# A ring of half-tick decays in PSUM, a second score bank, and operands laid out in half-tick slots

## The chip, the cores and the metric

The kernel runs on one core of one Trainium2 chip. The metric is the device time of one launch in microseconds (us), lower is better. The core has a matrix engine (TensorE, PE in the profile; its weight loads are listed apart as PEld), a vector engine (VectorE, DVE), an activation engine (ScalarE, ACT), a general engine (GpSimd, POOL) and a queue that issues transfers (SyncE, SP). Each engine takes its instructions strictly in the order in which they were written. Matrix products land in PSUM, eight banks of 128 partitions x 512 floats.

## The reference, cut to what matters

```python
# x: (4, 128, 64, 64): four images, 128 channels, 4096 pixels
x = x + attention(gn(x))        # 4096 x 4096 scores, softmax, values
x = x + conv5x5(gn(x))          # weights built from a radial table
x = x + ssm(gn(x))              # see below
x = x + conv3x3(gn(x))

# ssm: half of the channels runs forward over the pixels, half backward
xc    = silu(conv1d_4taps(Wx @ x))
delta = softplus(xc @ Wd + bd);  Bm = xc @ WB;  Cm = xc @ WC     # 64 states
h[t]  = exp(delta[t] * A) * h[t-1] + delta[t] * xc[t] * Bm[t]    # per channel and state
y[t]  = sum_n h[t, n] * Cm[t, n] + D * xc[t];  out = Wp @ y
```

`gn` is a group norm over 32 groups of 4 channels. All arithmetic is float32.

## The kernel before, in words

The scan of the state-space layer is the long part: 64 channels x 64 states x 2 directions are 64 sets of 128 rows, each 4096 pixels long, for four images. `scan_core` cuts this into **ticks**: one tick is one set of 128 rows over `CH` = 1024 pixels, 256 ticks an image, 1024 in all. A tick `i` has five steps, each on one engine:

- `drive(i + 2)`, L711, GpSimd: `db` = `dx` x `b` row (both in SBUF).
- `decay(i + 1, h)`, L704, ScalarE: `da` = exp(delta x A), written to PSUM. `da` has two buffers of two banks each, so a whole tick fits one buffer. While `attending` is set the decay is issued as two halves of 512, one at the tick's start and one in its middle, else as one instruction of 1024.
- `recur(i)`, L718 and L722, VectorE: a `tensor_tensor_scan` over 1024 pixels, and for 3 of 5 ticks (2 of 3 in the last image) the multiplication by the `c` row; in the other ticks GpSimd multiplies (`weigh`, L736).
- `keep(i - 1)`, L731, ScalarE: copies the last column of the state, the start value for the next 1024 pixels.
- `collect(i - 3)`, L750, TensorE: sums 4 states into a channel with 32-column products.

Everything else is written as generators. `front(b)` is attention, the 5x5 convolution and `scan_prep`/`scan_operands` of image `b`; `stage`, `end` and `back` finish an image after its scan. `front(0)` is written out first, alone. Then `scan_core` gives control away twice a tick, and the driver loop takes steps of the remaining work until their costs (the numbers that the generators yield: `PRODUCT` = 0.86 for one 128x512 product, `HOP` = 1.8 for a change of engine) have used up half of `pace`. `pace` is the summed cost of the first front divided by 248 ticks, so `front(b + 1)` is spread over the 256 ticks of image `b`. In the last image the pace is `ENDPACE` = 1.5 and the work is `stage`/`end`/`back` of the first three images.

PSUM before: 2 x 2 banks for `da`, and one bank each under the tags `s`, `a`, `z` and `y` (the last for `collect`).

**Attention** (L377 to L470) goes over 256 steps `u`, 32 blocks of keys for each of 8 blocks of queries: `scores(u)` (L380) multiplies into the bank `s`, ScalarE takes exp of it into an SBUF ring (L386), `values(u - 1)` (L392) adds the previous step's product to `a`, and every fourth step `sums` (L402) adds four steps' row sums in 32-column products. A float32 product is two matmul instructions with a weight load each. In TensorE's order a step is: scores(u), values(u - 1), sums now and then, and the scan's `y` products.

**Operands** (L538 to L651): for each of 8 pieces of 512 pixels, `taps` (16 matmuls into bank `s`), `halves` (L571, L572: half of the value to `xc`, tanh in place in PSUM), `silu` (L576, VectorE, from PSUM and `xc`), three products (L585: delta into `z`, the b and c rows one after the other into `a`), `softplus` (relu and abs, L598, L599), exp (L637), `digits` (L608 to L610) and two `row` copies (L590) with a DMA each. After the fourth and the eighth piece come the logarithms (L647, with a table load before and after) and `finish`: joins (L615), the DMA of delta, delta x xc on GpSimd into `xc` (L619) and its DMA. The next image's attention takes the buffer of `xc` (tag `A`) for its normalised input (L307).

Of the kernel before, what the change touches and what calls it, by code (L numbers as in the profile page):

```python
# [32 lines left out]
P = 128  # L33
# [10 lines left out]

PRODUCT, HOP, ENDPACE, SPARE, AHEAD = 0.86, 1.8, 1.5, 8, 4

# [5 lines left out]
def conv_preact_kernel(  # L52
# [36 lines left out]
    ps = ctx.enter_context(tc.tile_pool(name="ps", bufs=1, space=PSUM))  # L89
    pools, ready, attending = {}, set(), set()  # L90

    def bank(tag, name):
        return ps.tile([P, MM], F32, tag=tag, name=name)

# [172 lines left out]
    def group_norm(st, name):  # L267
# [29 lines left out]
        nc.vector.transpose(back.rearrange("p a b -> p (a b)"), after)  # L297
        yield HOP
        rs, nb = tile("rs", 1), tile("nb", 1)
        nc.gpsimd.tensor_tensor(rs, back[:, 0, 0:1], mhalf, ALU.pow)  # L300
        nc.gpsimd.tensor_tensor(nb, back[:, 1, 0:1], rs, ALU.mult)
        yield HOP
        yield HOP
# [15 lines left out]
    def attention(b, xs, gn, st, safe):  # L319
        xn = pools["big"].tile([P, ASIZE], F32, tag="A", name=f"xn0_{b}")[:, :L]  # L320
        for i in range(4):
            cut = bass.ts(i, L // 4)
            normalise(xn[:, cut], xs[:, cut], gn)
            yield HOP
        v = pools["big"].tile([P, VSIZE], F32, tag="V", name=f"v_{b}")
        v = v[:, : NJT * C].rearrange("p (j c) -> p j c", c=C)
        for i in range(NM):
            pv = bank("saz"[i % 3], f"pv_{b}_{i}").rearrange("p (t c) -> p t c", c=C)
            for t in range(TPM):
                nc.tensor.matmul(  # L330
                    pv[:, t, :], xn[:, bass.ts(i * TPM + t, P)], wv,
                    start=True, stop=True,
                )
            nc.scalar.copy(v[:, i * TPM : (i + 1) * TPM, :], pv)
            yield 2 * PRODUCT

# [40 lines left out]
        def scores(u):  # L377
            blk, j = divmod(u, NJT)
            sc = bank("s", f"sc_{b}_{u}")
            nc.tensor.matmul(sc, xn[:, bass.ts(j, P)], rq[blk], start=True, stop=True)  # L380
            pt = ring[:, u % NRING, :]
            if safe:
                nc.vector.tensor_tensor(pt, sc, mb[blk], ALU.subtract)
                nc.scalar.activation(pt, pt, AF.Exp)
            else:
                nc.scalar.activation(pt, sc, AF.Exp)  # L386
# [44 lines left out]
        def settle(blk):  # L431
# [6 lines left out]
            nc.vector.bn_stats(st[:, blk, :], xs[:, cut])  # L438

        queries(0)  # L440
        attending.add(b)
        for u in range(N + 7):
            blk, j = divmod(u, NJT)
            cost = 0.0
            if u < N:
                if safe and j == 0:
                    row_max(blk)
                scores(u)
                cost += PRODUCT
            if 0 < u <= N:  # L450
                values(u - 1)
                cost += PRODUCT
                d = (u - 1) % NJT
                if d == 3:
                    after(u, 3, sums, u - 1)
                elif d % 4 == 3:
                    sums(u - 1)
                    cost += PRODUCT
                if d == NJT - 1:
                    evict(blk - 1)  # L460
                    after(u, 2, turn, blk - 1)
                    after(u, 5, settle, blk - 1)
            if j == 16 and blk + 1 < NM:
                queries(blk + 1)
                cost += PRODUCT
            for f, args in later.pop(u, ()):
                f(*args)
                cost += PRODUCT
            yield cost or HOP
        attending.clear()  # L470


    def conv(b, xs, tag, st, weights, k, finish, name, residual=False):
# [16 lines left out]

        for i in range(2):
            piece(i)
            yield HOP
        done = None
# [26 lines left out]
    def scan_prep(b, xs, st, mats4):  # L521


        bc, dd, dxd, xcd, xsd = mats4
        pad = KC - 1
        xn = pools["big"].tile([P, VSIZE], F32, tag="V", name=f"xn2_{b}")
        nc.gpsimd.memset(xn[:, :pad], 0.0)
        nc.gpsimd.memset(xn[:, pad + L : 2 * pad + L], 0.0)
        gn = yield from group_norm(st, f"s{b}")

        for i in (0, 3, 1, 2):
            cut = slice(i * L // 4, (i + 1) * L // 4)
            normalise(xn[:, pad + cut.start : pad + cut.stop], xs[:, cut], gn)
            nc.sync.dma_start(xsd[:, cut], xs[:, cut])
            yield HOP
        return scan_operands(b, xn, mats4)

    def scan_operands(b, xn, mats4):  # L538

# [6 lines left out]
        delta = pools["big"].tile([P, L], F32, tag="xt", name=f"delta_{b}")  # L546
        pts, pzs, pbs, us = {}, {}, {}, {}

        def taps(i):
            pts[i] = pt = bank("s", f"pt_{b}_{i}")  # L550
            t = i * MM
            for k in range(KC):
                lo = L + 2 * pad - 1 - k - t - (MM - 1)
# [14 lines left out]
        def halves(i):  # L568

            pt = pts[i]  # L570
            nc.scalar.activation(xc[:, bass.ts(i, MM)], pt, AF.Identity, scale=0.5, bias=hbias)  # L571
            nc.scalar.activation(pt, pt, AF.Tanh, scale=0.5, bias=hbias)  # L572

        def silu(i):
            cut = bass.ts(i, MM)
            nc.vector.scalar_tensor_tensor(  # L576
                xc[:, cut], pts.pop(i), 1.0, xc[:, cut], ALU.add, ALU.mult
            )
# [32 lines left out]

        def finish(c):
            for i in range(c * CH // MM, (c + 1) * CH // MM):
                cut = bass.ts(i, MM)
                nc.vector.tensor_tensor(delta[:, cut], delta[:, cut], us.pop(i), ALU.add)  # L615
            cut = bass.ts(c, CH)
            nc.sync.dma_start(dd[c], delta[:, cut])
            yield HOP
            nc.gpsimd.tensor_tensor(xc[:, cut], delta[:, cut], xc[:, cut], ALU.mult)  # L619
            nc.sync.dma_start(dxd[c], xc[:, cut])  # L620
            yield HOP

        for i in range(NM + 1):
            if i < NM:
                taps(i)
                yield KC * PRODUCT
                halves(i)
            if i > 0:
                pzs[i - 1] = product(i - 1, 0, "z")
                yield PRODUCT  # L630
                pbs[i - 1, 1] = product(i - 1, 1, "a")
                softplus(i - 1)
            if i < NM:
                silu(i)
            if i > 0:
                yield PRODUCT
                nc.scalar.activation(pzs[i - 1], pzs[i - 1], AF.Exp, scale=-1.0)  # L637
                row(i - 1, 1)
                yield PRODUCT
                pbs[i - 1, 2] = product(i - 1, 2, "a")  # L640
                digits(i - 1)
                yield PRODUCT
                row(i - 1, 2)
            if i > 0 and i % HM == 0:
                yield HOP
                for n in range(i - HM, i):
                    nc.scalar.activation(us[n], us[n], AF.Ln)  # L647
                yield HOP
                for c in range((i - HM) * MM // CH, i * MM // CH):
                    yield from finish(c)  # L650
                ready.add((b, i))  # L651

# [3 lines left out]
    def scan_core(mats4, ynds, before):  # L656
# [5 lines left out]
        ]  # L662
        rows, rep, exps, dbs, hcs, hold, yacc, xcs, last = {}, {}, {}, {}, {}, {}, {}, {}, {}
        whole = {}

# [28 lines left out]

        def decay(i, h):

            b, c, d, q, g = ticks[i]
            if h == 0:
                exps[i] = ps.tile([P, CH], F32, tag="da", bufs=2, name=f"da_{i}")
                whole[i] = not attending  # L700
            elif whole.pop(i):
                return
            cut = slice(None) if h == 0 and whole[i] else bass.ts(h, MM)
            nc.scalar.activation(  # L704
                exps[i][:, cut], rep["de", b, c, d, g][:, cut], AF.Exp, scale=a_neg[:, at(i)]
            )
# [6 lines left out]
        def recur(i):  # L713
            b, c, d, q, g = ticks[i]
            hc = pools["hc"].tile([P, CH], F32, tag="hc", name=f"hc_{i}")
            da = exps.pop(i)
            h = hc if to_pool(i) else da
            nc.vector.tensor_tensor_scan(  # L718
                h, da, dbs.pop(i), 0.0 if c == 0 else last[b][:, at(i)], ALU.mult, ALU.add
            )  # L720
            if not to_pool(i):
                nc.vector.tensor_tensor(hc, h, rows["c", b, c, d, q], ALU.mult)  # L722
            hcs[i], hold[i] = hc, h

        def keep(i):
            b, c, d, q, g = ticks[i]
            h = hold.pop(i)
            if b not in last:
                last[b] = small.tile([P, NK * NQ], F32, tag="last", name=f"last_{b}")
            if c + 1 < NCH:  # L730
                nc.scalar.copy(last[b][:, at(i)], h[:, CH - 1 : CH])  # L731

# [294 lines left out]
```

## Time and profile before

| | |
|---|---|
| median of 3 runs | 5047.01 us (5046.7 to 5051.97) |
| the profiled execution | 5047.28 us, span of the profile 5045.2 us |
| instructions | 41640 |
| busy in the span | PE 86%, DVE 70%, ACT 45%, POOL 67% |
| granted TensorE clock | 0.928 |

The stages, by where the trace has the first and last instruction of each:

| stretch (us) | what runs |
|---|---|
| 0 to 40 | constants, first image, group norm, v of image 0 |
| 40 to 604 | attention of image 0, alone |
| 611 to 787 | 5x5 convolution of image 0, alone |
| 787 to 892 | operands of image 0, alone; the first tick's scan starts at 891.8 |
| 892 to 4116 | ticks of images 0, 1, 2, with the fronts of images 1, 2, 3 beside them: attention 898 to 1544, 1943 to 2592 and 2991 to 3638; convolution 1564 to 1773, 2618 to 2827 and 3662 to 3871; operands, group norms and the opening of attention between |
| 4116 to 4947 | ticks of image 3, with the ends of images 0 to 2 beside them |
| 4947 to 5045 | the end of image 3 alone |

Idle time of an engine costs something only where that engine sets the pace of its stretch; so the table of stretches has to be read with the busy time of each engine beside it. Matmuls are pipelined, so their recorded times overlap, and a busy PE can still lose time between two of them: for that the start times are to be compared.

### The profile page before, as it was taken

How to read it: one execution, taken by the hardware profiler on the slowest of the kernel's cores; microseconds unless marked ns; L12 is line 12 of the kernel's file. 1: busy time of each engine (PE TensorE's matmuls, PEld its weight loads, DVE VectorE, ACT ScalarE, POOL GpSimd, SP SyncE). 2: the span in 40 equal slices, each digit the busy share in tenths (PEclk: the TensorE clock that was granted, in tenths of full speed). 3: DMA queues.
4: the chain of work that ended last, by engine and by line, in shares of the span. 5: the costliest groups of instructions: out<-in, count | busy, mean ns of one | idle time of the engine just before them, and what ended most of it. 6: DMA issues, size and time to landing. Idle time of an engine off the chain costs nothing. (4 is left out here: it accounts for less than half of the span.)

```text
span 5045.2 us, 41640 instructions
## 1 busy us (share of the span) xinstructions
PE 4328.1 (86%) x14288; PEld 1484.1 (29%) x14288; DVE 3513.6 (70%) x2359; ACT 2261.0 (45%) x3843; POOL 3357.7 (67%) x1516
## 2 busy tenths in 40 slices
PE   7999996999998968999989869999999675858547
PEld 3333342333333312333323223333333121212102
DVE  5000003777778887777788887777788999999993
ACT  2322203655554345555553455555533544444331
POOL 0000000777778877777778777787788889999992
PEclk9999999999999989999999989999999797878668
DMA  1000003434444465444344554444444656565651
GB/s 44 0 0 0 0 4 118 162 135 144 151 148 149 152 215 177 149 139 153 130 156 149 193 186 145 144 149 144 151 156 165 248 179 225 196 229 201 209 189 49
DMA packets 208398, 710.90 MB, mean 141 GB/s; under 512 B 24624, under 2 KB 25520, under 8 KB 208048
## 3 DMA queue, kind: packets, MB, share of 16 engines
q1 hardware_dynamic: 206432, 706.83, 40.4%
q8 instruction: 114, 1.87, 0.2%
q10 hardware_dynamic: 1744, 1.32, 0.1%
q14 instruction: 108, 0.88, 0.1%
HBM read 640.94 MB, written 67.11 MB: 140 GB/s over the span
## 5 line engine op out<-in xcount | busy, mean ns | idle before, releaser
L711 POOL TENSOR_TENSOR db<-dx,br 128x1024 f32<-128x1024 f32 x1024 | 2405.3, 2364 | 597.0 <-DVE hc L718 255.2
L704 ACT ACTIVATE da<-de,a_neg 128x512 f32<-128x512 f32 (+1 forms) x1497 | 1267.4, 847 | 410.8 <-DVE hc L722 290.8
L718 DVE TENSOR_TENSOR_SCAN da<-da,last,db 128x1024 f32<-128x1024 f32 x474 | 1111.7, 2345 | 187.5 <-ACT da L704 167.9
L380 PE MATMUL sc<-r,xn 128*128 128x512 f32 x2048 | 1146.7, 642 | 40.2 <-ACT pt L386 19.7
L386 ACT ACTIVATE pt<-sc 128x512 f32<-128x512 f32 x1024 | 610.4, 596 | 1022.3 <-PE sc L380 1021.9
L392 PE MATMUL acc<-pt,v 128*128 128x512 f32 x2048 | 1046.4, 593 | 0.0
L750 PE MATMUL y<-hc,sel 128*32 128x512 f32 x4096 | 690.0, 675 | 409.0 <-POOL hc L736 379.5
L736 POOL TENSOR_TENSOR hc<-hc,cr 128x1024 f32<-128x1024 f32 x392 | 927.8, 2367 | 96.1 <-ACT last L731 93.0
L722 DVE TENSOR_TENSOR hc<-da,cr 128x1024 f32<-128x1024 f32 x632 | 774.1, 1225 | 54.0 <-issue 0.9
L502 PE MATMUL pce<-xpe,cw 128*128 128x512 f32 x1600 | 723.9, 606 | 40.0 <-ACT xpe L307 40.0
L718 DVE TENSOR_TENSOR_SCAN hc<-da,last,db 128x1024 f32<-128x1024 f32 x294 | 688.7, 2343 | 76.5 <-ACT da L704 51.7
L392 PEld LDWEIGHTS acc<-pt,v 128*128 128x128 f32 x2048 | 389.1, 190 | 491.4 <-issue 487.4
L380 PEld LDWEIGHTS sc<-r,xn 128*128 128x128 f32 x2048 | 305.2, 188 | 768.1 <-ACT pt L386 363.1
L718 DVE TENSOR_TENSOR_SCAN da<-da,db 128x1024 f32<-128x1024 f32 x158 | 361.9, 2290 | 147.1 <-ACT da L704 125.8
L502 PEld LDWEIGHTS pce<-xpe,cw 128*128 128x128 f32 x1600 | 298.6, 191 | 465.0 <-issue 420.9
L480 POOL MEMSET xpe<- 128x136 f32 x4 | 0.8, 211 | 569.1 <-PE sc L380 569.1
L750 PEld LDWEIGHTS y<-hc,sel 128*32 128x32 f32 x4096 | 103.6, 114 | 892.0 <-POOL hc L736 511.8
L426 DVE COPY zall<-pz 128x4 f32<-128x4 f32 x32 | 5.1, 160 | 497.6 <-PE pz L422 497.5
L731 ACT COPY last<-da 128x1 f32<-128x1 f32 x473 | 74.4, 157 | 576.4 <-DVE hc L722 575.7
L502 PE MATMUL pcm<-xpm,m 128*128 128x512 f32 x576 | 283.3, 640 | 23.5 <-ACT xpm L307 23.5
L402 PE MATMUL zp<-pt,ones 128*32 128x512 f32 x2048 | 272.7, 605 | 0.0
L718 DVE TENSOR_TENSOR_SCAN hc<-da,db 128x1024 f32<-128x1024 f32 x98 | 223.7, 2283 | 42.0 <-ACT da L704 34.2
(160 smaller groups left out, 1865.3 us busy)
## 6 DMA issues: line engine op xcount, KB each, us to landing
br<-bm SPq DMA_DIRECT2D x512, 512.0 KB, 5.1
cr<-cm SPq DMA_DIRECT2D x512, 512.0 KB, 4.0
de<-dd SPq DMA_DIRECT2D x64, 512.0 KB, 4.8
dx<-dxd SPq DMA_DIRECT2D x64, 512.0 KB, 6.1
x<-in_x_dram SPq DMA_DIRECT2D x16, 512.0 KB, 5.9
xsd<-x SPq DMA_DIRECT2D x16, 512.0 KB, 6.2
xcd<-xc SPq DMA_DIRECT2D x16, 512.0 KB, 2.7
bm<-bs SPq DMA_DIRECT2D x32, 256.0 KB, 2.2
```

Of the source, the lines that this page charges most:

```text
L380: nc.tensor.matmul(sc, xn[:, bass.ts(j, P)], rq[blk], start=True, stop=True)
L386: nc.scalar.activation(pt, sc, AF.Exp)
L392: nc.tensor.matmul(acc[blk], v[:, j, :], ring[:, u % NRING, :], start=j == 0, stop=j == NJT - 1)
L402: nc.tensor.matmul(zp[blk][g * 32 : (g + 1) * 32, :], ones[:, :32], ring[:, (u - 3 + g) % NRING, :], start=j == 3, stop=j == NJT - 1, tile ...
L502: nc.tensor.matmul(acc.rearrange("p (r w) -> p r w", w=W), weights[:, t, :], xp[:, y : y + RPM, dx : dx + W], start=t == 0, stop=t == k * ...
L704: nc.scalar.activation(exps[i][:, cut], rep["de", b, c, d, g][:, cut], AF.Exp, scale=a_neg[:, at(i)])
L711: nc.gpsimd.tensor_tensor(dbs[i], rep["dx", b, c, d, g], rows["b", b, c, d, q], ALU.mult)
L718: nc.vector.tensor_tensor_scan(h, da, dbs.pop(i), 0.0 if c == 0 else last[b][:, at(i)], ALU.mult, ALU.add)
L722: nc.vector.tensor_tensor(hc, h, rows["c", b, c, d, q], ALU.mult)
L731: nc.scalar.copy(last[b][:, at(i)], h[:, CH - 1 : CH])
L736: nc.gpsimd.tensor_tensor(hcs[i], hcs[i], rows["c", b, c, d, q], ALU.mult)
L750: nc.tensor.matmul(y[r : r + SG, :], sel, hcs[i - KG + 1 + gg][:, bass.ts(h, MM)], start=q == 0, stop=False, tile_position=(0, r), skip_gr ...
```

## The change

**PSUM.** `da` becomes one tile `ring4` of four banks. Where no front needs a bank (`borrowed` empty) a tick's decay is one instruction of 1024 and the two pairs of banks take turns. Where `borrowed` is set, a tick's decay is two halves in a ring of the first three banks, and the fourth, `s2`, is lent: in attention to every second `scores`, in the operands to every second delta product. `borrowed` is set from the start of an image's operands to the end of the next image's attention, and for the last image to the end of its operands. Before, the decay alone was cut, and only during attention.

**recur.** Where the decay is in halves, the scan and the multiplication are in halves too: scan, multiply, scan, multiply. The second scan starts from the last column of the first.

**Attention.** `values` and `sums` run two steps behind the scores (before: one). v is made in steps that interleave the four normalisations, the products and the copies.

**Operands.** They are written into slots of one `HOP` (now 1.7, about half a tick at this pace), a new piece every 5 slots, so that pieces overlap: a piece's `halves` is 4 slots behind its first taps, its `silu` 5, its products 8, 9 and 12, its `digits` 13. tanh goes to an SBUF tile (tag `w`) instead of back to its PSUM bank. delta x xc of the second half of the pixels goes to a buffer of tag `V`, not back into `xc`. Pieces 1 and 2 of the normalisation are written inside the slots.

**Yields.** Group norms yield once (before: three times), and the pieces before a convolution half a `HOP` (before: two).

```diff
-PRODUCT, HOP, ENDPACE, SPARE, AHEAD = 0.86, 1.8, 1.5, 8, 4
+PRODUCT, HOP, ENDPACE, SPARE, AHEAD = 0.86, 1.7, 1.5, 8, 4
+    ring4 = ps.tile([P, 4 * MM], F32, tag="da", name="ring4")
     def bank(tag, name):
+        if tag == "s2":
+            return ring4[:, 3 * MM :]
         return ps.tile([P, MM], F32, tag=tag, name=name)
...
         def scores(u):
             blk, j = divmod(u, NJT)
-            sc = bank("s", f"sc_{b}_{u}")
+            sc = bank(("s", "s2")[u % 2], f"sc_{b}_{u}")
...
-            if 0 < u <= N:
-                values(u - 1)
+            w = u - 2
+            if 0 <= w < N:
+                values(w)
...
         def halves(i):
-            pt = pts[i]
+            pt = pts.pop(i)
             nc.scalar.activation(xc[:, bass.ts(i, MM)], pt, AF.Identity, scale=0.5, bias=hbias)
-            nc.scalar.activation(pt, pt, AF.Tanh, scale=0.5, bias=hbias)
+            ths[i] = pools["bg"].tile([P, MM], F32, tag="w", bufs=4, name=f"th_{b}_{i}")
+            nc.scalar.activation(ths[i], pt, AF.Tanh, scale=0.5, bias=hbias)
...
+        def drives(c):
+            if c == NCH // 2:
+                late["dx"] = pools["big"].tile([P, VSIZE], F32, tag="V", name=f"dx_{b}")
             cut = bass.ts(c, CH)
+            dx = late.get("dx", xc)[:, cut]
+            nc.gpsimd.tensor_tensor(dx, delta[:, cut], xc[:, cut], ALU.mult)
+            nc.sync.dma_start(dxd[c], dx)
+        def delta_product(i):
+            pzs[i] = product(i, 0, ("z", "s2")[i % 2])
...
+        EVERY = 5
+        for i in range(NM):
+            t = EVERY * i
+            at(t, taps, i, 0, 1)
+            at(t + 1, taps, i, 2, 3)
+            at(t + 4, halves, i)
+            at(t + 5, silu, i)
+            at(t + 8, delta_product, i)
+            at(t + 9, row_product, i, 1)
+            at(t + 10, softplus, i)
+            at(t + 11, row, i, 1)
+            at(t + 12, exp, i)
+            at(t + 12, row_product, i, 2)
+            at(t + 13, digits, i)
+            at(t + 13, row, i, 2)
+        for i in (0, HM):
+            t = EVERY * (i + HM - 1) + 15
+            at(t, logs, i)
+            for n, c in enumerate(range(i * MM // CH, (i + HM) * MM // CH)):
+                at(t + 1 + n, join, c)
+                at(t + 3 + n, drives, c)
+            at(t + 3 + HM * MM // CH, ready.add, (b, i + HM))
...
+        borrowed.add(b)
+        for t in range(max(slots) + 1):
+            for f, args in slots.get(t, ()):
+                f(*args)
             yield HOP
...
         def decay(i, h):
+            if h == 0:
+                was = places.get(i - 1, [2])
+                if borrowed or was in ([1, 2], [2, 0]):
+                    first = (was[-1] + 1) % 3 if len(was) > 1 else (was[0] + 2) % 4
+                    places[i] = [first, (first + 1) % 3]
+                else:
+                    places[i] = [2 - was[0]]
+            if h == len(places[i]):
+                return
             b, c, d, q, g = ticks[i]
+            size = CH // len(places[i])
             nc.scalar.activation(
+                ring4[:, places[i][h] * MM :][:, :size],
+                rep["de", b, c, d, g][:, bass.ts(h, size)],
+                AF.Exp, scale=a_neg[:, at(i)],
             )
...
         def recur(i):
+            for n, place in enumerate(places[i]):
+                cut = bass.ts(n, size)
+                da = ring4[:, place * MM :][:, :size]
+                h = hc[:, cut] if to_pool(i) else da
+                nc.vector.tensor_tensor_scan(h, da, db[:, cut], before, ALU.mult, ALU.add)
+                before = h[:, size - 1 : size]
+                if not to_pool(i):
+                    nc.vector.tensor_tensor(
+                        hc[:, cut], h, rows["c", b, c, d, q][:, cut], ALU.mult
+                    )
+            hcs[i], hold[i] = hc, before
```

## The prediction

> **What bounds the kernel now.** I read the page's head first, then the table of stretches, because the page's 86% of PE is a mean over stretches with different limits.
>
> ```profile
> span 5045.2 us, 41640 instructions
> PE 4328.1 (86%) x14288; PEld 1484.1 (29%) x14288; DVE 3513.6 (70%) x2359; ACT 2261.0 (45%) x3843; POOL 3357.7 (67%) x1516
> ```
>
> The columns of the table of stretches are start:end, length, then busy us and count of PE, PEld, DVE, ACT and POOL, the granted clock, and the DMA.
>
> ```profile
> 40.00:600.00 560.00, 553.61 (x1662) 199.10 (x1662) 54.88 (x66) 166.69 (x279) 0.67 (x4) 1.00 0.00 0
> 898.00:1544.00 646.00, 638.34 (x2286) 215.01 (x2286) 485.76 (x283) 372.70 (x745) 508.59 (x219) 1.00 0.42 144
> 1544.00:1564.00 20.00, 6.99 (x42) 2.76 (x40) 16.56 (x22) 8.63 (x15) 13.79 (x12) 0.77 0.58 205
> 1564.00:1773.00 209.00, 208.88 (x624) 78.75 (x628) 172.59 (x103) 69.96 (x93) 177.76 (x79) 0.99 0.43 146
> 1773.00:1943.00 170.00, 101.87 (x395) 33.13 (x388) 151.68 (x127) 92.57 (x120) 123.17 (x56) 0.81 0.60 212
> ```
>
> Attention, alone (first line) and beside ticks (second), is PE's: 98.8% busy, with VectorE at 75%. So is the convolution. The group norms, operands and opening of attention (third and fifth) are VectorE's: 16.56 + 151.68 of 190 us, 89%, with PE at 57%. I call these two kinds **A** (attention, 646 to 649 us in each of three cycles) and **R** (the rest between: 20 + 170, 26 + 164, 24 + 149 = 553 us). The last image's 831 us (VectorE 804, GpSimd 792 busy) and the 98 us tail hold the same instructions before and after, since there the decays stay whole.
>
> A busy PE can still lose time between matmuls, so I looked at the timeline of attention alone (start, length, engine, operation, idle before and its releaser):
>
> ```profile
> 201.99 0.60 ACT L386 ACTIVATE pt<-sc 128x512 f32<-128x512 f32 x1 [1.22 <-PE sc L380]
> 202.64 0.30 PEld L380 LDWEIGHTS sc<-r,xn 128*128 128x128 f32 x2 [0.66 <-ACT pt L386]
> 202.65 1.12 PE L380 MATMUL sc<-r,xn 128*128 128x512 f32 x2
> 203.18 0.19 PEld L392 LDWEIGHTS acc<-pt,v 128*128 128x128 f32 x1 [0.24 <-issue]
> 203.60 1.02 PE L392 MATMUL acc<-pt,v 128*128 128x512 f32 x2
> ```
>
> The weight load for `acc` starts 0.42 us before its matmul, under the matmul ahead. The one for `sc` starts together with its matmul, because it waits for the exp that frees the bank (201.99 + 0.60 = 202.59). So a score pair takes 1.12 us where an `acc` pair takes 1.02: about 0.095 us from start to start, every time. The view of L380 says how often that wait ended last in this stretch:
>
> ```profile
>   ACT pt L386: 118.5, 179
> ```
>
> **The scores' second bank.** With `s` and `s2`, scores(u) needs exp(u - 2), over a step (1.8 us) earlier, and the load can go under the matmul ahead, as for `acc`. Alone: 179 x 0.095 = 17 us. The steps after `sums` keep their 1.13: their load starts late without waiting for ScalarE, after a 32-column product. Beside ticks, 131, 130 and 129 of 256 score pairs follow an `acc` matmul directly (in the trace's order): 12.4 us each; PE's idle before `sc` that ended with ScalarE's exp or `keep` (4.5 + 0.8, 8.2 + 0.8, 6.2 + 1.6) adds 5 to 9. That is 18, 21 and 20; I take 18 each: **-54**, and -17 for image 0. The cover: VectorE's 485.76 plus the halves below (154 ticks x 0.32 = 49) is 535 of 629 us, GpSimd's 509 is 81%, so PE stays the limit.
>
> **Operands of image 0, alone.** Start to start, pieces are 8.3 us apart:
>
> ```profile
> 801.67 3.65 PE L557 MATMUL pt<-xn,wtap 128*64 128x512 f32 x16 [2.18 <-DVE xc L576]
> 810.00 3.65 PE L557 MATMUL pt<-xn,wtap 128*64 128x512 f32 x16
> 818.32 3.65 PE L557 MATMUL pt<-xn,wtap 128*64 128x512 f32 x16
> ```
>
> In between PE waits for the chain product, ScalarE, product. In the new order PE does taps(i) (3.65), row 2 of i-2, delta of i-1 and row 1 of i-1 (about 0.95 each). taps(i+1) waits for `halves`(i), behind one row copy: 1.05 + 0.59 + 0.69 + 0.65 = 3.0 us after taps(i). So 6.6 apart, 1.7 x 7 = 12 us; the first wait for `silu` (2.2) goes, as tanh leaves the bank, and the chain after the last taps gets 1 shorter: **-15** (between -8, if the table loads of the logarithms, 2 x 1.28, come on the path, and -22). The first tick follows the last dx DMA as before.
>
> **R: the halves.** VectorE's groups, whole (count, then busy and mean ns):
>
> ```profile
> L718 DVE TENSOR_TENSOR_SCAN da<-da,last,db 128x1024 f32<-128x1024 f32 x474 | 1111.7, 2345 | 187.5 <-ACT da L704 167.9 <-POOL db L711 13.5 <-ACT last L731 5.5
> L722 DVE TENSOR_TENSOR hc<-da,cr 128x1024 f32<-128x1024 f32 x632 | 774.1, 1225 | 54.0 <-issue 0.9 <-PE y L750 0.5 <-DVE da L718 0.4
> L718 DVE TENSOR_TENSOR_SCAN da<-da,db 128x1024 f32<-128x1024 f32 x158 | 361.9, 2290 | 147.1 <-ACT da L704 125.8 <-ACT last L731 14.7 <-POOL db L711 6.5
> L615 DVE TENSOR_TENSOR delta<-delta,u 128x512 f32<-128x512 f32 x32 | 46.1, 1482 | 4.2 <-ACT u L647 4.2
> L436 DVE TENSOR_TENSOR pzb<-raw,pzb 128x512 f32<-128x512 f32 x32 | 22.2, 695 | 73.5 <-PE pzb L372 73.5
> ```
>
> A multiplication of 512 takes 695, of 1024 1225: an instruction more costs 2 x 695 - 1225 = 165 ns. No scan of 512 is in the trace. I give it the same 165, plus 55 for a start value read from memory (2345 - 2290): 0.22 + 0.6 x 0.165 = 0.32 us a tick, with 0 and 0.5 as bounds, since half the elements can't cost more than the whole and no row shows a larger fixed part. Ticks in R by the yields: 56 slots x 1.7 plus the opening of attention (21.75) over a pace of 3.31 are 35 for two cycles and 29 for the third, 99 in all: **+32** (0 to +50). A front costs 820.2 in yields after and 822.5 before, so the number of ticks beside each stage is the same within one.
>
> [...]
>
> **R: silu.** 24 of them beside ticks get both inputs from SBUF. Today one is in PSUM, and they take 687 ns. The join L615 has both in SBUF: mean 1482, up to 2845, when GpSimd works. 0 to 1.0 us each, since GpSimd is busy 72% here; I take 0.6: **+14** (0 to +24).
>
> [...]
>
> **R: waits that go.** VectorE is idle 51 of the 553 us (all six lines of R). In the first cycle 10.5 us of it wait for tanh (L572) ahead of `silu`; the slots put a half tick between. ScalarE waits 10.0 us for the DMA of dx before L307, with decays queued behind, and VectorE is idle 4.1 for that; after, xn waits for GpSimd's read of `xc` only. I take half of the 51: **-25** (-10 to -35).
>
> **Waits added.** In the ring, the second half of decay i+1 goes into the bank of tick i's first half, which the second scan still reads for its start value. Behind it on ScalarE are exps, operands and the next `keep`; PE waits for those. In A, VectorE runs half a tick ahead, so it has long been done. In R it costs nothing as long as VectorE has 2.6 us of other work (0.69 multiplication, 1.95 first half) before it needs that decay (0.69). GpSimd's two small group norm steps now wait for VectorE with drives queued behind; `db` is two ticks ahead, and I count 1 us each in the -25. SP issues as many DMAs as before; two xsd copies move into slots 1 and 2, ahead of the b and c rows, and nothing waits there for them. v's copies wait for dx of the second half, a few us after a HOP.
>
> **Sum.** -17 - 15 - 54 + 32 + 14 - 25 = -65. The profiled execution took 5047.28 (span 5045.2, 2.1 around it), 0.3 from the median of 5047.01, so 5047 - 65 = **4982**.
>
> **Rivals.** (1) *VectorE takes A over* (slower). If a half tick costs VectorE and its waits 1.2 us more, not 0.32, say because a decay half (0.69 plus a handover) is waited for in most ticks, then A needs 486 + 154 x 1.2 = 671 for 647, +24, and R 99 x 1.2 = 119 + 14 - 25 = +108: 3 x 24 + 108 - 32 = +148, 5195. A has room for 0.93 us a tick ((629 - 486) / 154), and from about there the whole is slower than before (-54 - 32 + 99 x 0.93 - 11 = -5). Against it: the 2.6 us of cover, and GpSimd and ScalarE below 82%. (2) *The load isn't pulled ahead*: the new load order, or exps delayed by decays, keep the 0.095. Then -15 and +21 are left, 5053, and without silu's contention 5040: no change. Against it: `acc` and the convolution (0.43 from start to start) do pull ahead. (3) *R gives all back*, halves at 0.5 and silu at 1.0, waits -10: +64 instead of +21: 5025, still faster.
>
> **How the numbers follow.** Measurement tells 0.2%, 10 us, from no change. Forecast with (3): 0.76; (1): 0.14; (2): 0.10, split between no change and both sides. The ends of the terms: -17 - 22 - 62 - 35 (R with halves and silu at nothing) gives 4911; half of A's gain (-36 with image 0), -8 and R at +64 give 5067. I cut these to 4925 to 5055, which takes in (2). Faster 0.77, same 0.08, slower 0.15.
>
> **What would show it.** Right: score pairs at 1.02 with their load 0.4 us ahead; attention alone 17 us shorter, beside ticks about 629; the first scan at about 860; scan halves near 1.28 us, R about 575 in all, `silu` above 1 us beside GpSimd. Wrong: A at 646 or above with VectorE over 90%, pairs still at 1.12, or R above 620.

## The result and the profile after

The changed kernel takes **7614.75 us** (median, 7609.04 to 7628.8), the kernel before 5046.85 beside it: 1.509 times as long, 95% interval 1.506 to 1.512. The forecast was 4982. The head of the page after the change:

```profile
span 7626.9 us, 43847 instructions
PE 5056.9 (66%) x14288; PEld 1719.8 (23%) x14288; DVE 3763.1 (49%) x3295; ACT 2322.4 (30%) x3955; POOL 3371.1 (44%) x1516
```

No engine is busy even two thirds of the time. The work of three engines is nearly what it was (VectorE 3763 us for 3514, ScalarE and GpSimd within 3%), so most of the 2.6 ms are waits. PE's matmuls, the same 14288, take 729 us more, at a lower granted clock (0.811 over the span for 0.928; last section). The table of stretches after says where (start:end, length, busy us and count of PE, PEld, DVE, ACT, POOL, then granted clock, DMA share, GB/s):

```profile
41.00:583.00 542.00, 535.92 (x1662) 213.54 (x1660) 54.01 (x65) 167.00 (x279) 0.66 (x4) 1.00 0.00 0
872.00:2157.00 1285.00, 829.09 (x2302) 274.30 (x2302) 541.17 (x532) 386.27 (x748) 508.97 (x218) 0.82 0.21 73
2178.00:2410.00 232.00, 220.49 (x618) 81.46 (x618) 165.73 (x98) 66.15 (x90) 164.46 (x71) 0.96 0.37 127
2410.00:2666.00 256.00, 125.73 (x400) 39.92 (x400) 184.25 (x191) 105.98 (x160) 140.42 (x65) 0.68 0.44 151
6333.00:7530.00 1197.00, 573.72 (x1524) 143.04 (x1526) 830.83 (x472) 350.45 (x505) 796.49 (x358) 0.67 0.41 142
```

The first line, attention alone, is shorter (560 before), as forecast. Everything with ticks in it is longer: attention beside ticks 1285 for 646 (second line), the convolution 232 for 209, the operands and group norms 256 for 170, and the last image 1197 for 831 (last line), though its decays are whole as before. VectorE, PE and GpSimd all stand still in the second line, VectorE for 744 us of 1285.

The list of waits of the whole span after (who waited for whom: total us, times, longest):

```profile
DVE ring L776 <- ACT ring L756: 1656.2, 582, 15.3
...
DVE hc L776 <- ACT ring L756: 1057.8, 352, 9.3
ACT ring L756 <- DVE hc L779: 1012.6, 296, 11.5
...
ACT last L790 <- DVE hc L779: 725.0, 194, 4.3
```

The same list of the kernel before, the longest waits of a scan for a decay and of a decay for a multiplication:

```profile
DVE da L718 <- ACT da L704: 293.7, 169, 15.6
ACT da L704 <- DVE hc L722: 290.8, 101, 10.4
```

After the change scans (L776) wait for decays (L756), and decays wait for VectorE's multiplications (L779), 5.6 and 3.5 times as long by the rows of the same kind. Each waits for the other: that is a chain, not a busy engine. The timeline of attention beside ticks shows its links (start, length, engine, operation, then in brackets the engine's idle time before it and what ended it):

```profile
1303.34 0.69 ACT L756 ACTIVATE ring<-de,a_neg 128x512 f32<-128x512 f32 x1
...
1304.12 1.22 DVE L776 TENSOR_TENSOR_SCAN hc<-ring,db 128x512 f32<-128x512 f32 x1 [4.41 <-ACT ring L756]
...
1305.38 1.28 DVE L776 TENSOR_TENSOR_SCAN hc<-ring,hc,db 128x512 f32<-128x512 f32 x1
...
1307.39 0.69 ACT L756 ACTIVATE ring<-de,a_neg 128x512 f32<-128x512 f32 x1
...
1309.92 0.69 ACT L756 ACTIVATE ring<-de,a_neg 128x512 f32<-128x512 f32 x1
...
1310.72 1.23 DVE L776 TENSOR_TENSOR_SCAN ring<-ring,db 128x512 f32<-128x512 f32 x1 [4.06 <-ACT ring L756]
...
1312.77 1.30 DVE L776 TENSOR_TENSOR_SCAN ring<-ring,db 128x512 f32<-128x512 f32 x1
1314.10 0.69 DVE L779 TENSOR_TENSOR hc<-ring,cr 128x512 f32<-128x512 f32 x1
...
1314.88 0.69 ACT L756 ACTIVATE ring<-de,a_neg 128x512 f32<-128x512 f32 x1 [3.28 <-DVE hc L779]
...
1315.63 1.12 PE L394 MATMUL ring<-r,xn 128*128 128x512 f32 x2 [3.80 <-ACT ring L756]
```

Call the scans at 1310.72 and 1312.77 tick j. Its two decay halves are the instructions at 1303.34 and 1307.39, done by 1308.08; VectorE had been free since 1306.66. Yet the scan starts only at 1310.72, right after the decay of 1309.92 ends at 1310.61. That decay is the first half of tick j + 1 and writes the third bank of the ring, which tick j doesn't touch. Then the next decay (1314.88) waits until the multiplication of 1314.10 has ended, although it writes a bank that this multiplication doesn't read (the scan of 1312.77, which takes its start value from that bank, was over at 1314.07). And the scores at 1315.63, which go to the fourth bank, lent to them alone, wait 3.80 us for that decay. So three engines with four banks take turns as if there were one.

The last image shows the same with nothing halved. First the kernel before, timeline near the end of the last image:

```profile
4701.29 2.34 DVE L718 TENSOR_TENSOR_SCAN hc<-da,last,db 128x1024 f32<-128x1024 f32 x1
...
4701.60 1.12 ACT L704 ACTIVATE da<-de,a_neg 128x1024 f32<-128x1024 f32 x1
4703.55 2.33 DVE L718 TENSOR_TENSOR_SCAN da<-da,last,db 128x1024 f32<-128x1024 f32 x1
```

The decay at 4701.60 runs under the scan of 4701.29, and the next scan follows at once. The changed kernel, same stage:

```profile
6902.85 2.36 DVE L776 TENSOR_TENSOR_SCAN ring<-ring,last,db 128x1024 f32<-128x1024 f32 x1 [0.76 <-ACT ring L756]
6905.30 1.22 DVE L779 TENSOR_TENSOR hc<-ring,cr 128x1024 f32<-128x1024 f32 x1
...
6906.81 1.12 ACT L756 ACTIVATE ring<-de,a_neg 128x1024 f32<-128x1024 f32 x1
...
6908.03 2.36 DVE L776 TENSOR_TENSOR_SCAN ring<-ring,last,db 128x1024 f32<-128x1024 f32 x1 [1.50 <-ACT ring L756]
```

No decay starts until scan and multiplication are over, and no scan until the next decay is over. From scan to scan a tick of the last image takes 4.64 us on average, before 3.25.

**Theories.** T1: the four banks are *one tile* (one named piece of memory that the program declares; the kernel's text holds no waits, so those of the trace are put in for it), and in this program an access to a tile in PSUM is ordered behind the last access to any part of it. T2, nearest to rival (1) of the prediction: the ring's true needs cost this, since the second half of a decay needs the bank of the tick before. T3: the engines collide in neighbouring banks. T2 and T3 don't explain the last image well, but only a run decides.

### The profile page after: what moved, and what is told of

Its sections match the earlier page's. It is cut to its first block, busy times and chain, and to the rows that moved or that the text cites. A ratio compares the mean times of both kernels' runs of the same rounds, so it can differ in the third digit from the quotient of the medians.

```text
span 7626.9 us, 43847 instructions
## 1 busy us (share of the span) xinstructions
PE 5056.9 (66%) x14288; PEld 1719.8 (23%) x14288; DVE 3763.1 (49%) x3295; ACT 2322.4 (30%) x3955; POOL 3371.1 (44%) x1516
## 5 line engine op out<-in xcount | busy, mean ns | idle before, releaser
L756 ACT ACTIVATE ring<-de,a_neg 128x512 f32<-128x512 f32 (+1 forms) x1609 | 1299.1, 807 | 1505.5 <-DVE hc L779 1012.6
L394 PE MATMUL ring<-r,xn 128*128 128x512 f32 x1024 | 750.4, 823 | 1351.8 <-DVE hc L779 570.9
L776 DVE TENSOR_TENSOR_SCAN ring<-ring,last,db 128x512 f32<-128x512 f32 (+1 forms) x474 | 865.4, 1826 | 1130.9 <-ACT ring L756 1118.1
L776 DVE TENSOR_TENSOR_SCAN ring<-ring,db 128x512 f32<-128x512 f32 (+1 forms) x509 | 695.3, 1366 | 550.4 <-ACT ring L756 538.1
L776 DVE TENSOR_TENSOR_SCAN hc<-ring,last,db 128x512 f32<-128x512 f32 (+1 forms) x294 | 523.1, 1779 | 724.1 <-ACT ring L756 706.3
L779 DVE TENSOR_TENSOR hc<-ring,cr 128x512 f32<-128x512 f32 (+1 forms) x983 | 829.9, 844 | 67.4 <-DVE ring L776 2.3
L400 ACT ACTIVATE pt<-ring 128x512 f32<-128x512 f32 x512 | 305.7, 597 | 1447.6 <-PE ring L394 1447.6
L394 PE MATMUL sc<-r,xn 128*128 128x512 f32 x1024 | 616.2, 686 | 15.6 <-ACT r L363 14.0
L400 ACT ACTIVATE pt<-sc 128x512 f32<-128x512 f32 x512 | 304.0, 594 | 789.3 <-PE sc L394 789.1
L776 DVE TENSOR_TENSOR_SCAN hc<-ring,db 128x512 f32<-128x512 f32 (+1 forms) x98 | 142.3, 1452 | 353.2 <-ACT ring L756 351.4
L776 DVE TENSOR_TENSOR_SCAN hc<-ring,hc,db 128x512 f32<-128x512 f32 x234 | 300.1, 1283 | 8.3
```

The source lines that it names most:

```text
L756: nc.scalar.activation(ring4[:, places[i][h] * MM :][:, :size], rep["de", b, c, d, g][:, bass.ts(h, size)], AF.Exp, scale=a_neg[:, at(i)],)
L776: nc.vector.tensor_tensor_scan(h, da, db[:, cut], before, ALU.mult, ALU.add)
L779: nc.vector.tensor_tensor(hc[:, cut], h, rows["c", b, c, d, q][:, cut], ALU.mult)
```

## The experiments

**1. Four tiles.** Only the declaration of the ring, and with it that a whole decay, which can't span two tiles, becomes two halves everywhere:

```diff
-    ring4 = ps.tile([P, 4 * MM], F32, tag="da", name="ring4")
+    ring4 = [ps.tile([P, MM], F32, tag=f"da{k}", name=f"ring4{k}") for k in range(4)]
...
-            return ring4[:, 3 * MM :]
+            return ring4[3]
...
-                da = ring4[:, place * MM :][:, :size]
+                da = ring4[place]
```

> The changed kernel with its ring as four separate tiles of one bank instead of one tile of four banks; nothing else of the order changes, except that a whole decay (last image, and wherever the changed kernel keeps decays whole) is also issued as two halves. Theory T1 (one tile of four banks is waited for as one, so that decays, scans and scores take turns): the waits go, and the time falls to the forecast plus the added halves of the last image: 4982 plus up to 256 ticks x 0.32 = 82, so 5000 to 5070. Attention beside ticks falls from about 1280 us to about 629. Theory T2 (the true needs of the ring: the second half of a decay needs the bank of the tick before, VectorE takes attention over): nothing of that is changed, 7550 to 7700, attention beside ticks stays near 1280. Theory T3 (ScalarE, VectorE and TensorE collide in neighbouring banks, whatever the tiles): the same 7550 to 7700, or a little more.

Measured 5056.65 us, 1.0014 [1.0005, 1.0024] times before. 2558 us are gone; the ring's needs, its order and its halves are all still there. T2 and T3 fall.

**2. Four tiles, then two.** As the first, but ahead of the last image's first decay the four one-bank tiles are given back and two tiles of two banks taken, so that this image has whole decays as in the kernel before:

```diff
+            if i + 1 == LAST:
+                do(recur, i)
...
+                ringpool.close()
+                pools["whole"] = whole.enter_context(
+                    tc.tile_pool(name=f"whole{mode[0]}", bufs=2, space=PSUM)
+                )
+                do(decay, i + 1, 0)
```

> As the kernel with four separate tiles, but before the last image's first decay the four banks are given back and taken again as two tiles of two banks each, so that the last image has whole decays in two places, as in the kernel before. T1: the forecast itself, 4960 to 5010, the last image at about 831 us as before. T2 and T3: the last image is freed (about 7530 - 6333 = 1197 us falls to 831), the rest stays: 7250 to 7350.

Measured **4984.12 us** (4983.19 to 4985.05), 0.9871 [0.9854, 0.9887] times before: close to the forecast time. It is nearly the change as forecast, but not quite: its ticks are halved between the ring's stages too, where the changed kernel keeps them whole. The three convolutions take 629 us here and 625 in experiment 7, where their ticks are whole. Its table of stretches:

```profile
870.00:1501.00 631.00, 626.64 (x2302) 226.57 (x2302) 524.63 (x532) 372.70 (x748) 509.35 (x219) 1.00 0.43 149
1501.00:1519.00 18.00, 3.48 (x28) 2.09 (x24) 16.51 (x27) 6.29 (x13) 10.94 (x11) 0.74 0.52 175
...
1729.00:1904.00 175.00, 104.29 (x394) 33.38 (x394) 169.48 (x190) 101.78 (x158) 134.99 (x60) 0.82 0.60 212
...
4054.00:4884.00 830.00, 499.66 (x1523) 126.92 (x1521) 802.61 (x471) 350.67 (x504) 792.95 (x354) 0.75 0.59 205
```

Attention beside ticks has the same 532 VectorE and 2302 PE instructions as after, in 631 us instead of 1285. Its timeline shows the three engines in three of the banks at once:

```profile
1310.90 0.69 ACT L762 ACTIVATE ring_False<-de,a_neg 128x512 f32<-128x512 f32 x1
1310.97 1.02 PE L395 MATMUL ring_False<-r,xn 128*128 128x512 f32 x2
...
1311.51 1.27 DVE L785 TENSOR_TENSOR_SCAN hc<-ring_False,last,db 128x512 f32<-128x512 f32 x1
```

The scan begins at 1311.51, before the decay ends (1311.59) and while the scores are written (until 1311.99).

**3. The kernel before with one tile.** The test from the other side: nothing of the change but the declaration.

```diff
+    ring4 = ps.tile([P, 2, CH], F32, tag="da", name="ring4")
...
-                exps[i] = ps.tile([P, CH], F32, tag="da", bufs=2, name=f"da_{i}")
+                exps[i] = ring4[:, i % 2, :]
```

> The kernel before with one edit: its two places for decays, two tiles of two banks, become one tile of four banks whose halves are used in turn. No ring, no halves, no second bank for scores. T1: decays and scans take turns here too. In the last image a tick then costs a decay, its handover and the scan with its multiplication, about 3.97 us as in the changed kernel for 3.25, +185 us there; beside attention and in the rest VectorE has less to do and part of it hides: 5600 to 6600 in all. T2 and T3: the needs between instructions are those of the kernel before, 5030 to 5065.

Measured 6174.08 us, 1.2228 [1.2208, 1.2248]. One tile in place of two costs 1124 us in a kernel that has no ring and no second bank for scores. The waits turn the same way:

```profile
ACT ring L705 <- DVE hc L723: 1182.6, 382, 8.7
...
DVE ring L719 <- ACT ring L705: 1015.3, 578, 16.4
```

The last image's tick takes 4.65 us, as in the changed kernel (4.64). My 3.97 for it was too small; the direction and the total stand.

**4. Which users of the tile cost what.** The second experiment's kernel, its three ring banks one tile again, the lent bank a tile of its own:

```diff
+            three = rp.tile([P, 3 * MM], F32, tag="da0", name=f"ring_{safe}")
+            ring4[:] = [three[:, bass.ts(k, MM)] for k in range(3)]
+            ring4.append(rp.tile([P, MM], F32, tag="da3", name=f"ring3_{safe}"))
```

> The kernel of the second experiment (separate tiles, whole decays for the last image) with one edit: the ring's three banks are one tile again, the lent bank stays a tile of its own. T1: decays and scans of the ring take turns, but the scores no longer stand in that line. A tick then costs two half decays, two half scans, the multiplications and the handovers, 1.38 + 2.56 + 0.62 x 1.38 + 0.3 = 5.1 us, up to 5.7 with exps between the decays; 768 such ticks instead of 3195 us in all take 3900 to 4400, so 5700 to 6150 in all. What is missing from there to the changed kernel (its last image apart) would be the scores' share. If the scores' bank alone were the cause (T1b), this kernel stays within 1% of 4984. T2 (true needs) is out.

Measured 5951.4 us, 1.1788 [1.177, 1.1806]. The waits in its first attention beside ticks, 874 us long:

```profile
ACT ring_False L762 <- DVE hc L788: 327.8, 88, 4.3
DVE ring_False L785 <- ACT ring_False L762: 177.2, 83, 5.1
ACT ring_False L762 <- DVE hc L785: 138.5, 60, 2.8
```

With 154 ticks in each such stretch, a tick takes 4.1 us with separate tiles, 5.7 with the ring as one, and 8.3 in the changed kernel, where the scores stand in line too. So of the 2631 us between the changed kernel and the second experiment, the ring's own turns are 5951 - 4984 = 967; the last image, where the pairs are in one tile, 1197 - 830 = 367; and the rest, about 1300, is left for the scores and delta products in the same tile. That last part is had by subtraction alone. T1b, that the lent bank is the whole cause, falls: it was the largest part, not the only one.

**5. One bank for all scores.** The second experiment's kernel with one edit:

```diff
-            sc = bank(("s", "s2")[u % 2], f"sc_{b}_{u}")
+            sc = bank("s", f"sc_{b}_{u}")
```

> The kernel of the second experiment with one edit: all scores go into bank s again, none into the lent bank. Forecast's step (the weight load waits for the exp, 0.095 us a pair, 17 us alone and some 18 a cycle): pairs at 1.12 us again, attention of image 0 17 us longer, attention beside ticks 646 instead of 632, 5035 to 5055 in all. Rival (the gain came from values running two steps behind the scores, not from the bank): below 5000.

Measured 5114.93 us, 1.0132 [1.0117, 1.0148]: 131 us more than the second experiment where I expected 51 to 71. Attention alone, from the first scores to the end of the last value product, is 559.6 us for 540.8, 19 longer where 17 were expected. Beside ticks it is 666 to 670 for 631 to 633, +36 a cycle and not +14. The group of `sc` in the first of these stretches:

```profile
L395 PE MATMUL sc<-r,xn 128*128 128x512 f32 x512 | 291.8, 652 | 19.1 <-ACT last L799 10.7 <-ACT pt L401 6.0 <-ACT r L364 2.3
```

With two banks PE's idle before scores is 5.1 in that stretch, with one 19.1, most of it ended by `keep` (L799). `keep` waits on ScalarE for VectorE (in the kernel before `ACT last L731 <- DVE hc L722`: 575.7 us in 264 waits), and the exps that free the one bank are written behind it. So beside ticks the second bank also absorbs ScalarE being late; with halves and one bank attention is longer than before the change (666 for 646). In this stretch PE is busy 647 us for 627 and idle 14 more before scores, which together are its 35. Of the 20 of busy time the load's 0.095 us makes about 12 (an estimate, for 130 pairs as in the prediction); the rest goes with a granted clock of 0.98 instead of 1.00.

**6. tanh back in PSUM.**

```diff
-            ths[i] = pools["bg"].tile([P, MM], F32, tag="w", bufs=4, name=f"th_{b}_{i}")
+            ths[i] = pt
```

> The kernel of the second experiment with one edit: tanh overwrites the bank of the taps again instead of going to SBUF, so silu has one input in PSUM. Forecast's step (silu with both inputs in SBUF is slowed beside GpSimd, 24 x 0.6 = 14 us): 4965 to 4980, silu at about 0.69 us. Rival (VectorE and GpSimd don't slow each other here, or the bank held until silu makes the taps wait): 4984 to 5000.

Measured 4978.21 us (4977.03 to 4978.89), 5.9 less than the second experiment (the kernel before ran 1.5 faster beside it, so 4 to 6). VectorE's group for `silu`, the second experiment first, then this one:

```profile
L601 DVE SCALAR_TENSOR_TENSOR xc<-th,xc 128x512 f32<-128x512 f32 x32 | 43.7, 1367 | 22.0 <-ACT th L597 22.0
```

```profile
L601 DVE SCALAR_TENSOR_TENSOR xc<-pt,xc 128x512 f32<-128x512 f32 x32 | 21.8, 681 | 34.3 <-ACT pt L597 19.8 <-PE pb L610 14.5
```

22 us of VectorE's work go and 12 of new idle come. Both theories are partly right.

**7. The ring in attention alone.** Outside attention two tiles of two banks and whole decays; seven changes of pool in all, each as in the second experiment; `settled(i)` is `keep(i)`, issued while its bank is still held.

```diff
     def scan_operands(b, xn, mats4, piece):
...
-        borrowed.add(b)
...
+            if (mode[-1] == "ring") != bool(borrowed):
+                do(recur, i)
+                do(settled, i)
+                switch("ring" if borrowed else "whole")
+                do(decay, i + 1, 0)
```

> The kernel of the second experiment with the ring used during attention alone: at its start and end the four banks are given back and taken anew, as four tiles of one bank or two of two; outside attention every decay, scan and multiplication is whole, and the delta products use one bank. Forecast's step (a halved tick costs VectorE 0.32 us more, 99 ticks in R): 32 us less, of which six changes of pool, each a decay that can't be issued ahead (about 1.3 us), give back 4 in R: 4950 to 4965. Rival (the halves are hidden in R too, or the single delta bank costs as much as it frees): 4980 to 5000.

Measured 4964.3 us (4959.7 to 4969.51), 0.9835 [0.9822, 0.9849]: 20 less than the second experiment, at the upper end of what was expected. The operands' stretch that took 175 us in the second experiment:

```profile
1729.00:1898.00 169.00, 106.01 (x403) 35.17 (x402) 164.75 (x133) 94.29 (x122) 133.40 (x60) 0.78 0.62 219
```

All six pieces of R are 546 us for 571; attention beside ticks gives back 5 us a cycle (636 to 638). That is 10; the other 10 lie outside A and R, 4 of them in the convolutions, where the second experiment has halves and this one whole ticks.

**8. Both of these together.**

> The two edits that helped, together: the ring in attention only, and tanh back in the bank of the taps. If they add, 4964.3 - 5.9 = 4958, range 4954 to 4964. Rival (with VectorE less late in R, the bank held until silu costs as much as silu gains): 4964 to 4970. Both kernels, before and changed, would be slower than this one.

Measured **4957.43 us** (4955.35 to 4960.39), 0.9822 [0.9808, 0.9835] times before. The gains add (4958 expected), and this is the fastest of all versions run: 90 us under the kernel before.

**9. One tile of three axes.** The changed kernel with the tile declared `[P, 4, MM]` and its banks taken as `[:, k, :]`.

> The changed kernel with its ring as one tile of three axes, 128 x 4 x 512, indexed by the bank, in place of 128 x 2048 cut by columns. T1, if the order is kept for a tile as a whole however it is cut: 7550 to 7700. T1c (the order goes by an axis where there is one): as with four tiles, 4980 to 5070.

One run, 7622.61 us: no difference. Of the two ways to cut the tile neither helps; that it is one tile is what counts.

## Why the prediction was wrong, point by point

**The step that failed** is "Waits added". It took the instruction order, asked for each decay half which bank it overwrites and who still reads that bank, and found that VectorE is done in time. It never asked what unit the order is kept in. It read "a ring of the first three banks" as three buffers; in the program they are one tile. The trace of before has no decay and scan in two parts of one PSUM tile (each place for a decay was a tile), so this was an operation that the trace doesn't show, and it was put at nothing instead of being bounded. The bound was at hand: if decay, scan, multiplication and scores take turns, a tick in A costs at least 2 x 0.69 + 2 x 1.28 + 0.6 x 1.38 = 4.8 us and the handovers, more than the 4.2 that A has (648 / 154), so the whole would be slower. The prediction's first step carried the same oversight, "hold the same instructions before and after" of the last image: true (472 instructions on VectorE for 469), and yet 366 us wrong, as its two places had become one tile as well.

What hides it is that another ring in the same kernel, `pt` in SBUF, is also one tile with slots, and ScalarE writes one slot while PE reads another (in attention alone after the change, an exp at 204.03 under the `acc` products of 203.83 to 204.85). From the form of the code the two look alike. Yet the scores in the fourth bank, which no decay writes during attention, wait 3.80 us for one (the row at 1315.63), and in experiment 2 these accesses overlap (the decay from 1310.90 to 1311.59, the scores from 1310.97 to 1311.99). What had to wait and what the program made wait were different things here, and the second sets the time.

**The rivals.** Rival (1) had the right sign and place (a decay half that is waited for in most ticks) and the wrong engine: VectorE was to be full, and it is 42% busy in A. Its 5195 is 2400 us off. Rivals (2) and (3) are not what happened. The three hold no case in which the order itself is coarser than the buffers.

**The other steps**, read in the second experiment, whose profiled span is 4982.7 us for 5045.2, -62.5:

- *Second score bank, alone* (-17): attention alone, from the first scores to the end of the last value product, 540.8 us after and with separate tiles, for 558.8 before: -18. Right. The pair's load goes under the matmul ahead, here in the changed kernel's timeline, 0.43 us early:

```profile
204.26 0.19 PEld L394 LDWEIGHTS ring<-r,xn 128*128 128x128 f32 x1 [0.24 <-issue]
204.69 1.02 PE L394 MATMUL ring<-r,xn 128*128 128x512 f32 x2
```

- *Operands alone* (-15): pieces were to be 6.6 us apart. In the changed kernel's timeline of the taps they are 6.56:

```profile
793.99 3.65 PE L580 MATMUL pt<-xn,wtap 128*64 128x512 f32 x16
800.55 3.65 PE L580 MATMUL pt<-xn,wtap 128*64 128x512 f32 x16
```

  The first scan starts at 858.2 (after) and 859.1 (second experiment); forecast "about 860", before 891.8. From the end of attention to the first scan it is 277 us for 293, -16. Right.
- *Attention beside ticks* (-54): 631 + 633 + 632 for 646 + 649 + 647 is -46, forecast 629 each. Right within 8. Why it is right was not quite: the fifth experiment puts the second bank itself at 36 a cycle, and the rest of the change in A at about +21 against it (its 666, 670 and 669 for 646, 649 and 647), a loss that I had not priced.
- *R, halves* (+32): half scans and half multiplications in the second experiment:

```profile
L788 DVE TENSOR_TENSOR hc<-ring_False,cr 128x512 f32<-128x512 f32 x922 | 638.0, 692 | 55.1 <-issue 0.9
...
L785 DVE TENSOR_TENSOR_SCAN hc<-ring_False,hc,db 128x512 f32<-128x512 f32 x307 | 393.9, 1283 | 89.0 <-ACT ring_False L762 62.8
```

  1283 ns for the forecast 1.28 us. A halved tick costs (5056.65 - 4984.12) / 256 = 0.28 us in the last image (forecast 0.32), and taking the halves out of R brings 25 us there (experiment 7, with its changes of pool). Right within 7.
- *R, silu* (+14): of the 24 beside ticks 7 take 0.67 to 0.68 us in the second experiment as ever, the others up to 2.77; together 37.0 us for 16.4, +21. The term was too small: 17 pay, 1.2 us each on average, not 24 with 0.6. Which ones pay shows in the trace of the second experiment, here one case of each kind:

```profile
2843.25 2.34 POOL L774 TENSOR_TENSOR db<-dx,br 128x1024 f32<-128x1024 f32 x1 [3.38 <-DMA dx<-dxd]
2843.37 2.77 DVE L601 SCALAR_TENSOR_TENSOR xc<-th,xc 128x512 f32<-128x512 f32 x1
...
3842.33 0.67 DVE L601 SCALAR_TENSOR_TENSOR xc<-th,xc 128x512 f32<-128x512 f32 x1
3842.56 2.66 POOL L774 TENSOR_TENSOR db<-dx,br 128x1024 f32<-128x1024 f32 x1 [1.53 <-DVE hc L785]
```

  Each of the 17 starts while a GpSimd instruction runs and ends about 0.54 us after that one. Of the 7 others one meets no GpSimd instruction, and six start 0.22 us or so ahead of one, which then takes some 0.3 us longer. So in these 23 pairs the one that started second took longer: `silu` 17 times, up to 2.77 us for 0.67, GpSimd's instruction six times, 2.66 us for 2.34 in the rows above.
- *R, waits that go* (-25): VectorE's idle in R is 22 us for 51, -29. Right. R in all: 571 for 553, +18, forecast +21 and 575.

So each term that came from a row of the trace held within some 10 us, in the second experiment together to 2 us by luck of signs, and the one that came from an assumption on the program was off by 2631.

## What to carry to other kernels

Before buffers are merged into one tile, ask in what unit the program orders accesses to it: here, banks of one PSUM tile took turns, and four one-bank tiles of the same size gave back 2558 us. When several engines stand idle at once and the list of waits shows two of them waiting for each other, look for a shared object, and compare the addresses that waiter and releaser touch: a wait between two that share no data, as the 3.80 us of the scores for a decay here, points at the object, not at the data. Cutting work to free a buffer can be confined to the stage that needs the buffer: the ring in attention alone beat halves in all of the first three images by 20 us.

## What the runs showed of the hardware

The granted clock of PE fell with its idle time in attention beside ticks: 1.00 with separate tiles (idle 4 of 631 us), 0.94 with the ring as one tile (179 of 874), 0.82 after the change (456 of 1285). The same `acc` products in that stretch, the second experiment, the fourth and the changed kernel in turn:

```profile
L407 PE MATMUL acc<-pt,v 128*128 128x512 f32 x512 | 261.1, 592 | 0.0
```

```profile
L407 PE MATMUL acc<-pt,v 128*128 128x512 f32 x512 | 283.6, 638 | 8.9 <-ACT raw L427 3.8 <-ACT pt L401 3.6 <-ACT last L799 1.4
```

```profile
L406 PE MATMUL acc<-pt,v 128*128 128x512 f32 x512 | 333.9, 742 | 0.0
```

592, 638 and 742 ns times the clock is 592, 600 and 608: the work is the same within 3%, the clock slower. PE is 829 us busy in A after the change for 627 with separate tiles, so in these three runs the waits of PE came with longer matmuls, a second cost. How much of these 202 us lies on the chain was not separated from the waits. Nor do the runs say why the order is kept by tile in PSUM and by slot in the SBUF ring.
